# A graph layer on one core: spare rows gathered for two sets at once, 105 sets in place of 107, and another way to split x

## The chip, the core and the metric

The kernel runs on one core of a Trainium2 chip. The metric is the device time of one execution in microseconds (us): before the change the median of three runs is 1756.15 us (1748.27 to 1756.86). A profiled execution of the same kernel took 1757.87 us, and its span, from the first to the last instruction, is 1756.1 us.

The engines have short names in the profile. PE is the matrix engine (PEld its weight loads), DVE the vector engine, ACT the scalar engine, POOL the GpSimd engine. SP issues most DMA transfers, ACT and POOL issue some. An engine carries out its instructions strictly in the program's order, so an instruction that waits holds up everything behind it on its engine.

## The reference

```python
Xs = X[src]                                            # 400000 edges, 12500 nodes, 128 features
m_data = Xs @ W_data.T + b_data
m_ctrl = Xs @ W_control.T + b_control
msg = jnp.where((edge_types == 0)[:, None], m_data, m_ctrl)
agg = jax.ops.segment_sum(msg, dst, num_segments=X.shape[0])
out = relu(agg + (X @ W_self.T + b_self))
result = layernorm(X + out)
```

The edges are sorted by `dst`. Since the weights are the same for all edges of a type, the kernel sums the raw rows `X[src]` by destination and type first, and multiplies the sums by the weights afterwards.

## The kernel before, in words

**x in three parts.** Each f32 number of x is kept as three bf16 parts whose sum is the number, in SBUF as `x3` (128 partitions, 98 blocks, 3 parts, 128 features) and in DRAM as `rows3`. `split_x` makes the parts piece by piece, 14 blocks to a piece: ACT copies x to the first part (L262), DVE subtracts it from x (L263), ACT copies the rest to the second part (L264), DVE subtracts again into the third (L265). Seven full or nearly full pieces and one of 84 rows are made in the prologue. `store_rows` writes them to `rows3` (L269).

**Two ways to fetch rows.** The 3125 chunks of 128 edges fall into 25 groups of 125. Some chunks are *gathered*: an indirect DMA that POOL issues brings one `rows3` row per edge into a `msg` tile (`fetch`, L754). The others come in *sets* of 20 chunks (2560 edges) that PE serves: the edges are sorted into cells of 32 by the block of x in which their source lies, a 0/1 matrix `pick` is made, and PE multiplies it with `x3` (`pick`, L820) to get the rows; ACT brings them from PSUM to SBUF (`emsg`, L834). How many sets a group has is decided by `sets(g)`: five where g is a multiple of 4, else four, which makes 107 sets and 985 gathered chunks.

**Sums by destination.** For both kinds a 0/1 matrix (`psel`, `esel`, made by `select` on DVE, L504) says which destination and type a row belongs to, and PE multiplies (L704); counts go the same way (L842, L790). DVE adds a window of sums to the group's accumulator `acc` (L743). Finished tiles of 125 destinations are multiplied by the weights, normalized and written (`finish_batch`).

**A set in steps.** `give_slots` plans one set, ahead of its use: `block_matrix` (`O`, which block each edge's source is in), `fours` and `same_lane`, `before` (PE sums of who comes first, L584), `ranks` (each edge's place in its cell), `rank_matrix` (`rm`, `rv`), `over`, then `put` (L647), `spread` (the cells go through DRAM, `there`, and come back to all partitions as `pick`), `turn_codes` and `keep_codes`. `pick_matrix` turns the broadcast into the 0/1 matrix (L690). `picked` then works through the set in five turns: in each turn PE fetches four or five cells' rows (two in one PSUM tile, the rest in another), ACT evicts them, and PE counts and adds those of the turn before; `end` adds the last ones during the first turn of the next set.

**Spare rows.** A cell holds 32 edges. Edges over that, up to 64 a set, are *spare*: `over` finds them (up to seven a partition), `spare_slots` gives each a place: `over_before` (one PE matmul, L520), `over_matrix` (DVE, `om_all`, L526), `turn` (seven PE matmuls, L530), `keep` (three ACT copies, the last of which makes the row numbers `idx`, L541). `spare_rows` gathers these rows with one indirect DMA of 64 rows per set (L798) into the lower half of the tile `last`; its upper half takes the rows of two cells that are fetched by PE (L836). The last sum of the set reads `last`. The spare slots of set w are made while set w + 1 is planned, and the gather is issued in the second turn of set w.

**What sets the order.** The order of work on each engine is mostly written out: `merged` interleaves lists of units by numbers between 0 and 1. POOL's gathers are paced: `due` gives each a time in sets, and `paced` ties it to a matmul (a gate). 14 gathers run ahead (`AHEAD`), 18 `msg` tiles exist (`HOLD`). `issue_after` puts instructions behind a given one in their engine's order. The PSUM tile `side` exists once and is taken in turn by many steps.

**The prologue.** Before the first set can run, the tables are made, group 0 is loaded and prepared (`prep_e`), x is split, and sets 0 and 1 are planned. PE's first L820 starts at 68.00 us, POOL's first gather at 68.07 us.

Of the kernel before, what the change touches and what calls it, by code (L numbers as in the profile page):

```python
# [10 lines left out]
I32 = mybir.dt.int32  # L11
AF = mybir.ActivationFunctionType
# [138 lines left out]
def short_path(ctx, tc, const, ident, eps, wT, brow, bad, x, src, dst, etype, ws, bs, out):  # L151
# [24 lines left out]
    def sets(g):  # L176

        return NE if g % 4 == 0 else NE - 1
# [66 lines left out]
    def split_x(pool):  # L245
# [13 lines left out]
        def split(b, m, rows):  # L259
            t = tiles.pop(b)  # L260
            h, mm, lo = (x3[:rows, b:b + m, j, :] for j in range(3))
            nc.scalar.copy(h, t)  # L262
            nc.vector.tensor_sub(t, t, h)  # L263
            nc.scalar.copy(mm, t)  # L264
            parted.append(nc.vector.tensor_sub(lo, t, mm))  # L265
# [10 lines left out]
        for k, p in enumerate(pieces):  # L276
            def unit(k=k, p=p):
                split(*p)
# [25 lines left out]
    cell_col = keep.tile([P, NCELL], BF, name="cell_col")  # L304
    nc.vector.tensor_copy(cell_col.rearrange("p (a q) -> p a q", q=NQ), iota([4, NQ], [[1, 4], [4, NQ]], 0, 0, "i0"))
    for a, b in ((0, -1.0), (1, -1.0), (2, 96.0), (3, 97.0)):
        nc.vector.memset(cell_col[:, a * NQ + NQ - 1:a * NQ + NQ], b)
# [27 lines left out]
    om_all = keep.tile([P, TOP + 1, OVF], BF, name="om_all")  # L335
    nc.vector.memset(om_all, 0.0)
# [7 lines left out]
    for a in range(4):  # L344
        nc.vector.tensor_scalar(ltri[:, a, :], free[:, a, :], own_f[:, a:a + 1], None, op0=OP.is_gt)
# [10 lines left out]

    halves = tmp.tile([1, 2, NG * NE], I32, name="halves")
    nc.vector.memset(x3[:, NBLK - 1], 0.0)
    first = first_i["e"].rearrange("o g w -> o (g w)")
    nc.vector.tensor_single_scalar(halves[:, 0, :], first, 7, op=OP.logical_shift_right)  # L360
    nc.vector.tensor_single_scalar(halves[:, 1, :], first, 127, op=OP.bitwise_and)
# [12 lines left out]
    def places_and_weights():  # L374
        near = raw["near"] = keep.tile([rows_p, NG], FP, name="near")
        from_i = tmp.tile([rows_p, 1], I32, name="from_i")
        from_f = tmp.tile([rows_p, 1], FP, name="from_f")
        nc.gpsimd.iota(from_i, pattern=[[0, 1]], base=-PAD, channel_multiplier=DPC)
        nc.vector.tensor_copy(from_f, from_i)
        for k in range(1, NE):  # L380
            ge = raw[f"ge{k}"] = tmp.tile([rows_p, 1], FP, name=f"ge{k}")
            nc.vector.tensor_scalar(
                ge, from_f, float(DPC * PB * k - PAD), float(-DPC * PB), op0=OP.is_ge, op1=OP.mult
            )
        for k in range(1, NE):
            nc.vector.tensor_add(from_f, from_f, raw.pop(f"ge{k}"))
# [5 lines left out]
        least = tmp.tile([1, NG, NWIN], FP, name="least")  # L392
        for i, (_, _, c, _) in enumerate(windows(0)):
            nc.vector.memset(least[:, :, i:i + 1], float(max(0, c * DPC - PAD)))
# [80 lines left out]
    def prep_e(g):  # L475
# [17 lines left out]
        for v, val in enumerate((parts[:, 1, :], code)):  # L493
            nc.scalar.copy(vals2[:, :, v, :], val.rearrange("p (n o) -> p n o", o=1).to_broadcast([P, n, 2]))
        codes["e", g] = (blk, twice("blk2", parts[:, 0, :]), vals2, pk)

# [15 lines left out]
    def spare_slots(w, at):  # L512

# [3 lines left out]
        s = slots[w]  # L517

        def over_before():
            nc.tensor.matmul(  # L520
                at["ahead"][:, 500:501], ltri[:, 0, :], over_n[:, w:w + 1], start=True, stop=True, skip_group_check=True
            )

        def over_matrix():
            s["om"] = om_all.rearrange("p k o -> p (k o)")
            nc.vector.tensor_scalar(om_all[:, :TOP], slot_col, at["ahead"][:, 500:501], None, op0=OP.is_equal)  # L526

        def turn():
            for k in range(TOP):
# [719 lines left out]
```

## Time and profile before

| What | us |
|---|---|
| median of three runs | 1756.15 |
| profiled execution, its time | 1757.87 |
| its span | 1756.1 |
| ACT busy, of the span | 1229.2 (70%) |
| POOL, L754, 985 gathers of 128 rows, busy | 1190.9 |
| PE, L820, 10486 picks, busy | 568.0 |
| ACT, L834, 1070 evictions, busy | 951.9 |

How to read the rows that the prediction shows. A group of instructions is `line engine op out<-in shapes xcount | busy us, mean ns | idle before, and what ended it`. A timeline row is `start us, us, engine line op names xcount [idle before <-releaser]`; several like instructions in a row are merged, so that the time from one row's start to the next is what the engine spent on them. A row of the waits is `who waited <- for whom: us in total, times, longest us`. A row of a source line gives the count, then shortest, median and longest duration in ns, and the starts of the first and the last one. A row of the windows gives a stretch, its length and each engine's busy time in it, with the number of instructions that started there. Matmul ends are modelled and overlap; their starts are what counts.

### The profile page before, as it was taken

The page shows a single profiled execution, that of the slowest core. Times are in us where ns is not written, and L with a number is a line of the kernel's source. Part 1 is how long each engine was busy: PE and PEld are TensorE (multiplying, and loading weights), DVE is VectorE, ACT ScalarE, POOL GpSimd, SP SyncE. Part 2 cuts the span into 40 slices and gives each one's busy share as a digit, 9 for nine tenths or more (in the row PEclk, how much of TensorE's full clock was granted, in tenths as well). Part 3 has the DMA queues.
Part 4 walks back from the last instruction along what each step waited for, and adds up shares of the span by engine and source line. Part 5 has one row for each costly group of instructions (what it writes and reads, how often), then busy time and mean ns, then how long its engine had stood idle before and what let it go on. Part 6 is the DMA issues. An engine that isn't in the chain of part 4 may idle for free.

```text
span 1756.1 us, 72083 instructions
## 1 busy us (share of the span) xinstructions
PE 1615.3 (92%) x29945; PEld 1311.7 (75%) x29945; DVE 1595.2 (91%) x3996; ACT 1229.2 (70%) x2249; POOL 1316.6 (75%) x1109
## 2 busy tenths in 40 slices
PE   0599999999999999999999999999999989999997
PEld 0377777777778777777877877777777777878786
DVE  8899999998999998999988999999999989999993
ACT  4577777767677667767766777776777766767675
POOL 0288877787777787877887877887877877777871
PEclk9999999999999999999999999999999999999999
DMA  8655454446454545444535454544454535544441
GB/s 237 209 165 160 128 158 136 147 125 199 115 164 134 159 125 179 143 152 127 166 119 164 150 164 133 164 122 147 160 159 135 158 108 162 167 139 141 151 139 41
DMA packets 190562, 261.28 MB, mean 149 GB/s; under 512 B 86437, under 2 KB 155983, under 8 KB 187152
## 3 DMA queue, kind: packets, MB, share of 16 engines
q1 hardware_dynamic: 126894, 148.02, 25.9%
q0 software_dynamic: 50704, 102.16, 20.8%
q10 hardware_dynamic: 12626, 6.40, 1.2%
q8 instruction: 236, 3.87, 0.9%
q14 instruction: 102, 0.84, 0.1%
HBM read 238.47 MB, written 18.00 MB: 146 GB/s over the span
## 4 chain that ended last, share of the span: by engine, by line
PE 48%; DVE 32%; issue 6%; DMA 6%; ACT 5%; DVEq 1%; POOL 1%; SPq 0%; POOLq 0%; ACTq 0%
PE sums L704 22%; PE got L820 15%; DVE esel L504 3%; PE side L950 3%; DVE pick L690 3%; PE sums L842 3%; DMA last<-rows,idx 3%; DVE rv L635 2%; ACT emsg L834 2%; DVE prod L598 2%; DVE prod L576 2%; PE side L584 2%; DVE acc L743 2%; PE side L647 2%; DVE ahead L594 2%
## 5 line engine op out<-in xcount | busy, mean ns | idle before, releaser
L754 POOL DMA_INDIRECT msg<-rows,pidx x985 | 1190.9, 1209 | 307.5 <-issue 118.9
L834 ACT CAST emsg<-got 128x768 bf16<-128x768 f32 (+1 forms) x1070 | 951.9, 930 | 303.9 <-PE got L820 289.8
L704 PE MATMUL sums<-esel,emsg 128*128 128x176 bf16 x7704 | 683.4, 240 | 0.0
L704 PEld LDWEIGHTS <-emsg 128*128 128x128 bf16 x7704 | 566.9, 98 | 68.7 <-issue 28.5
L820 PE MATMUL got<-x,pick 128*32 128x384 bf16 x10486 | 568.0, 330 | 21.9 <-DVE pick L690 14.7
L820 PEld LDWEIGHTS <-pick 128*32 128x32 bf16 x10486 | 239.2, 96 | 139.2 <-issue 20.6
L504 DVE TENSOR_TENSOR esel<-code_col,code 128x1760 bf16<-128x1760 bf16 x321 | 292.7, 912 | 13.6 <-PE sums L704 11.6
L798 POOL DMA_INDIRECT last<-rows,idx x107 | 122.0, 1141 | 106.0 <-DVE pick L690 63.7
L704 PE MATMUL sums<-psel,msg 128*128 128x48 bf16 x2955 | 184.2, 184 | 17.2 <-DVE acc L743 15.2
L842 PE MATMUL sums<-esel,one_col 128*32 128x176 bf16 x2675 | 193.7, 240 | 4.4 <-DVE acc L743 4.4
L704 PEld LDWEIGHTS <-msg 128*128 128x128 bf16 x2955 | 149.9, 97 | 36.2 <-issue 31.4
L842 PEld LDWEIGHTS <-one_col 128*32 128x32 bf16 x2675 | 111.9, 97 | 60.7 <-issue 4.1
L790 PE MATMUL sums<-psel,one_col 128*128 128x48 bf16 x985 | 150.2, 183 | 0.0
L743 DVE TENSOR_TENSOR acc<-acc,sums 128x352 f32 (+2 forms) x232 | 99.4, 430 | 40.4 <-PE sums L704 36.8
L504 DVE TENSOR_TENSOR O<-cell_col,blk 128x2000 bf16<-128x2000 bf16 x107 | 128.2, 1198 | 2.1 <-issue 2.1
L598 DVE TENSOR_TENSOR prod<-O,ahead 128x2000 bf16<-128x2000 bf16 x107 | 127.6, 1193 | 0.1
L690 DVE TENSOR_SCALAR pick<-pick,lane_f 128x3200 bf16<-128x3200 bf16 x107 | 113.2, 1058 | 0.0
L647 PE MATMUL side<-rv,O 128*128 128x64 bf16 x2140 | 83.3, 195 | 31.6 <-DVE rv L635 30.6
L647 PEld LDWEIGHTS <-O 128*128 128x128 bf16 x2140 | 78.7, 100 | 33.3 <-DVE rv L635 29.3
L594 DVE TENSOR_REDUCE ahead<-side 128x100 bf16<-128x500 f32 x107 | 72.2, 675 | 28.0 <-PE side L520 27.3
L790 PEld LDWEIGHTS <-one_col 128*128 128x128 bf16 x985 | 94.3, 96 | 0.0
L635 DVE TENSOR_TENSOR rv<-rm,vals 128x1280 bf16<-128x1280 bf16 x107 | 87.8, 821 | 0.3
(170 smaller groups left out, 1869.2 us busy)
## 6 DMA issues: line engine op xcount, KB each, us to landing
pick<-there SPq DMA_DIRECT2D x107, 800.0 KB
acc<-acc_start SPq DMA_DIRECT2D x23, 1280.0 KB
msg<-rows,pidx POOLq DMA_INDIRECT x985
rows<-x SPq DMA_DIRECT2D x6, 1344.0 KB
xs<-in_x_dram SPq DMA_DIRECT2D x99, 62.5 KB
out_dram<-h SPq DMA_DIRECT2D x99, 62.5 KB
xt<-in_x_dram ACTq DMA_DIRECT2D x6, 896.0 KB
there<-cell SPq DMA_DIRECT2D x107, 6.2 KB
```

What stands on the lines that cost most here:

```text
L504: nc.vector.tensor_tensor(sel.rearrange("p n (w t) -> p n w t", t=2), col[:rows].rearrange("p (o w t) -> p o w t", o=1, t=2).to_broadcast( ...
L598: nc.vector.tensor_tensor(prod, s["O"], ahead.rearrange("p (o j) -> p o j", o=1).to_broadcast([P, EC, NCELL]), op=OP.mult)
L635: placed[:] = [nc.vector.tensor_tensor(rv.rearrange("p c v (r t) -> p c v r t", t=2), rm.rearrange("p c (o r t) -> p c o r t", o=1, t=2).t ...
L647: nc.tensor.matmul(s["rk"][:m, :2 * CAP], s["held"][:, c * NCELL:c * NCELL + m], s["rv"][:, c].rearrange("p v r -> p (v r)"), start=(c == ...
L690: nc.vector.tensor_scalar(t, t, lane_f, None, op0=OP.is_equal)
L704: last = nc.tensor.matmul(out, msg[:, j * D:(j + 1) * D], sel, start=(start and j == 0), stop=stop, skip_group_check=True)
L743: added.append(nc.vector.tensor_add(win, win, ps[:, :4 * wide].rearrange("p (a w) -> p a w", w=wide)[:, :, :width]))
L754: return nc.gpsimd.indirect_dma_start(out=msg, out_offset=None, in_=rows3[:, :], in_offset=bass.IndirectOffsetOnAxis(ap=codes["p", g][0][: ...
L790: nc.tensor.matmul(cnt, one_col, sel, start=False, stop=(c == n - 1), skip_group_check=True)
L820: last = nc.tensor.matmul(ps[CAP * a:CAP * (a + 1), :], slots[w]["pick"][:, a * NQ + q, :], x3[:, 4 * q + a - a0].rearrange("p j d -> p (j ...
L834: nc.scalar.copy(msg[:, :n], ps[:, :n, :3 * D])
L842: nc.tensor.matmul(cells_of(s["ps"], EW, 1)[CAP * (q % 4):CAP * (q % 4 + 1), :], one_col[:, :CAP], s["sel"][q], start=(q < 4), stop=(q + 4 ...
```

## The change

Five things change together.

1. `sets(g)` gives five sets where g is a multiple of 6, four elsewhere: 105 sets and 1025 gathered chunks.
2. The spare rows of two neighbouring sets, an even and the following odd one, come with one indirect DMA of 128 rows into `both`. The even set's spare slots are made as before; the odd set's are made from its own `rk` tile (`own_before`, `own_turn`). Of the even set, ACT copies its 64 rows from `both` to `last` at the end of the set's last turn; for the odd set `both` itself serves as `last`. The odd set has the halves of the tile, and the cells at its ends (`cell_cols`), the other way round. `both` and `last` have one buffer each.
3. x's parts are taken from its bytes: the upper two bytes of a f32 number are the first part, a bf16 number as they stand. ACT copies them, and copies the two lower bytes as numbers times 2^-15 and 2^-23; DVE masks sign and exponent out of the first part (`power`) and multiplies both other parts by it.
4. In the prologue, tables and the starting points of the gathered windows are made on DVE before the work that needs group 0's first loads; group 0's `prep_e` comes ahead of the split on ACT; the preparations of later groups stand behind `placed`.
5. The first set's two transfers `there` and `pick` are issued on POOL's queue.

```diff
-        return NE if g % 4 == 0 else NE - 1
+        return NE if g % 6 == 0 else NE - 1
...
-            h, mm, lo = (x3[:rows, b:b + m, j, :] for j in range(3))
-            nc.scalar.copy(h, t)
-            nc.vector.tensor_sub(t, t, h)
-            nc.scalar.copy(mm, t)
-            parted.append(nc.vector.tensor_sub(lo, t, mm))
+            part = x3[:rows, b:b + m]
+            byte = t.bitcast(U8).rearrange("p k (d b) -> p k d b", b=4)
+            nc.scalar.copy(part[:, :, 0, :], t.bitcast(BF).rearrange("p k (d b) -> p k d b", b=2)[:, :, :, 1])
+            for j in range(2):
+                nc.scalar.activation(part[:, :, 2 - j, :], byte[:, :, :, j], AF.Copy, scale=2.0 ** (8 * j - 23))
+            power = pool.tile([P, step, D], BF, name="power", bufs=2)[:rows, :m, :]
+            nc.vector.tensor_single_scalar(
+                power.bitcast(I16), part[:, :, 0, :].bitcast(I16), -128, op=OP.bitwise_and
+            )
+            parted.append(nc.vector.tensor_tensor(
+                part[:, :, 1:, :], part[:, :, 1:, :],
+                power.rearrange("p k (j d) -> p k j d", j=1).to_broadcast([rows, m, 2, D]), op=OP.mult,
+            ))
...
-    def spare_slots(w, at):
+    def spare_slots(w, at, col=504):
...
-        s = slots[w]
-
-        def over_before():
+        s, k = slots[w], w % 2
+        half = slice(k * OVF, k * OVF + OVF)
+        om = om_all[k]
+
+        def over_before(to="ahead", c=500):
+            s["before"] = at[to][:, c:c + 1]
...
-            spares = s["spares"] = spare_slots(w - 1, s)
+            spares = s["spares"] = spare_slots(w - 1 if w % 2 else -1, s)
...
+            queue = nc.sync if w else nc.gpsimd
+            queue.dma_start(out=there[:, :], in_=cell[:NCELL, :CAP])
...
+        def own_before():
+            s["own"] = spare_slots(w, s, 509)
+            s["own"][0]("rk", 508)
+            s["own"][1]()
+
+        def own_turn():
+            s["own"][2]()
+            s["own"][3]()
+
         s["tiled"] = {4: [put, spread], 5: [turn_codes, keep_codes]}
+        if w % 2:
+            s["tiled"][5] = [lambda: (turn_codes(), own_before()), keep_codes]
+            s["own_turn"] = own_turn
...
     def spare_rows(w):
-        msg = slots[w]["last"] = two.tile([P, 3 * D], BF, name="last")
+        n = P if w + 1 < pairs else OVF
+        both = two.tile([P, 3 * D], BF, name="both", bufs=1)
+        slots[w + 1 if n == P else w]["last"] = both
+        if n == P:
+            slots[w]["both"] = both
         return nc.gpsimd.indirect_dma_start(
-            out=msg[:OVF, :], out_offset=None, in_=rows3[:, :],
-            in_offset=bass.IndirectOffsetOnAxis(ap=slots[w]["idx"], axis=0),
+            out=both[:n, :], out_offset=None, in_=rows3[:, :],
+            in_offset=bass.IndirectOffsetOnAxis(ap=slots[w]["idx"][:n], axis=0),
         )
...
-            if t == 1 and w > 0:
+            if t == 1 and w > 0 and w % 2 == 0:
                 spare.append(lambda: spare_rows(w))
             if t == 3:
                 assert not spare
+                if "both" in slots[w]:
+                    slots[w]["last"] = two.tile([P, 3 * D], BF, name="last", bufs=1)
...
+            if t == 0 and w + 1 < pairs and "own_turn" in slots[w + 1] and w > 0:
+                slots[w + 1]["own_turn"]()
+            if t == turns - 1 and "both" in slots[w]:
+                nc.scalar.copy(slots[w]["last"][:OVF, :], slots[w]["both"][:OVF, :])
...
+    with tc.issue_after(tables.ins):
+        ready = prep_e(0)
     split_units.pop(0)()
-    prep_e(0)
```

More of the change, by code (lines that the diff above doesn't have):

```diff
@@ L344, in short_path @@
     for a in range(4):
[L345 removed]
+        tables = nc.vector.tensor_scalar(ltri[:, a, :], free[:, a, :], own_f[:, a:a + 1], None, op0=OP.is_gt)
     one_col = keep.tile([P, P], BF, name="one_col")
@@ new lines, in keep @@
+            nc.scalar.copy(
+                code, at["rk"][half, col + 2:col + 3].rearrange("p (n o) -> p n o", o=1).to_broadcast(list(code.shape))
+            )
+            part = two.tile([P, 2], FP, name="part")
+            nc.scalar.copy(part[half], at["rk"][half, col:col + 2])
+            if k == 0:
+                s["idx"] = two.tile([P, 1], I32, name="idx")
+            idx = slots[w - k]["idx"][half]
+            nc.scalar.activation(idx, part[half, 0:1], AF.Identity, bias=part[half, 1:2], scale=128.0)
@@ L1064, in ending, with later @@
         pass
+    def later(g):
+        with tc.issue_after(placed[0].ins):
+            prep_e(g)
     for w in range(pairs):
```

106 lines of the change are left out of this document (56 added, 50 removed).

## The prediction

> **What bounds the kernel now.** I read the page for the totals, then a window of the steady stage, then POOL's own timeline, then the waits.
>
> ```profile
> span 1756.1 us, 72083 instructions
> ...
> PE 1615.3 (92%) x29945; PEld 1311.7 (75%) x29945; DVE 1595.2 (91%) x3996; ACT 1229.2 (70%) x2249; POOL 1316.6 (75%) x1109
> ...
> L754 POOL DMA_INDIRECT msg<-rows,pidx x985 | 1190.9, 1209 | 307.5 <-issue 118.9 <-PE got L820 80.5 <-PE sums L704 51.9
> ```
> ```profile
> core 0: us, PE busy (x) PEld busy (x) DVE busy (x) ACT busy (x) POOL busy (x), PEclk, DMA share, GB/s
> 800.00:1000.00 200.00, 190.94 (x3583) 155.77 (x3576) 184.38 (x466) 142.73 (x267) 160.68 (x130) 1.00 0.48 144
> ```
> ```profile
> 889.76 1.04 POOL L754 DMA_INDIRECT msg<-rows,pidx  x1 [0.30 <-PE got L820]
> 891.10 3.51 POOL L754 DMA_INDIRECT msg<-rows,pidx  x1 [0.30 <-PE sums L704]
> 894.92 3.01 POOL L798 DMA_INDIRECT last<-rows,idx  x1 [0.30 <-ACT emsg L834]
> 898.24 0.95 POOL L754 DMA_INDIRECT msg<-rows,pidx  x1 [0.30 <-issue]
> ...
> 900.09 0.40 PE L704 MATMUL sums<-esel,last 128*128 128x176 bf16 x3 [3.04 <-DMA last<-rows,idx]
> ...
> 895.02 1.84 ACT L834 CAST emsg<-got 128x768 bf16<-128x768 f32 x2
> ...
> 900.69 0.20 ACT L677 CAST code<-side 128x50 bf16<-128x50 f32 x1 [3.83 <-PE side L530]
> ```
> ```profile
> PE sums L704 <- DMA last<-rows,idx: 15.2, 11, 4.5
> ```
>
> By its busy share POOL looks free (75%). It isn't. In the timeline every gather starts 0.30 us after the one before has ended, whichever releaser is named. In the 200 us window POOL has 130 gathers: 130 x 0.30 = 39 us of pauses and 160.7 us of work make 199.7 of 200 us. So POOL runs back to back, with PE at 95% and DVE at 92% beside it: three engines that are nearly equally full. What ties PE to POOL is the spare gather (`last`): when POOL lags, it lands late and PE stands still, as at 900.09 for 3.04 us; there were 11 such waits, 15.2 us in all. A change must lighten all three to gain its full worth.
>
> **The change, part by part.**
>
> *Sets and chunks.* Sets go from 107 to 105 (groups of five sets: 7 of 25 before, 5 of 25 after), chunks that POOL gathers from 985 to 1025. Gathers of spare rows go from 107 with 64 rows to 52 with 128 rows and one with 64.
>
> ```profile
> L754 POOL DMA_INDIRECT msg<-rows,pidx x985: 942/1043/4798, 73.2 to 1720.5; - x197
> ```
> ```profile
> L798 POOL DMA_INDIRECT last<-rows,idx x107: 911/1059/3007, 68.1 to 1729.9; - x107
> ```
> ```profile
> L798 POOL DMA_INDIRECT last<-rows,idx x107 | 122.0, 1141 | 106.0 <-DVE pick L690 63.7 <-issue 17.7 <-ACT idx L541 11.5
> ```
>
> POOL: 985 + 107 = 1092 slots become 1025 + 53 = 1078. If all take the mean of a 128-row gather, 1.209 us, busy time goes from 1190.9 + 107 x 1.14 (122.0 us) = 1312.9 to 1303.3, -9.6 us, and 14 pauses of 0.30 fall away, -4.2: together -14 us. If a wide spare gather is no dearer than a narrow one (the medians, 1059 ns for 64 rows and 1043 for 128, say so), 14 average slots of 1.50 go: -21 us.
>
> The spread of `msg` (0.94 to 4.8 us for the same 128 rows) is no cost of the gather alone. The Trainium skill ("SBUF — State Buffer", section "SBUF: two separate sides") says that VectorE's two-port instructions and GpSimd exclude each other from a shared port, so that descriptors which GpSimd writes must wait. By that rule only the shortest time is the gather's own, 14 x (0.94 + 0.30) = 17.4 us are saved by count, and the rest of POOL's time belongs to VectorE's work by set, 2 sets of it: (1312.9 - 1092 x 0.94) / 107 x 2 = 5.4 us, -22.7 us in all by this estimate. The 3.51 us gather above agrees with waiting of some kind, but names no port.
>
> PE: one set's matmuls are read from starts in the timeline.
>
> ```profile
> 808.06 1.00 PE L820 MATMUL got<-x,pick 128*32 128x384 bf16 x20
> 808.88 0.32 PE L842 MATMUL sums<-esel,one_col 128*32 128x176 bf16 x5
> 809.13 0.41 PE L584 MATMUL side<-prod,ltri 128*128 128x125 bf16 x4
> ...
> 809.41 1.30 PE L704 MATMUL sums<-esel,emsg 128*128 128x176 bf16 x15
> 810.54 0.24 PE L704 MATMUL sums<-psel,msg 128*128 128x48 bf16 x3
> ...
> 810.83 1.00 PE L820 MATMUL got<-x,pick 128*32 128x384 bf16 x20
> ```
>
> 20 picks take 0.82 us to the next start, so 98 take 4.0; 5 counts 0.25, so 25 take 1.25; 15 sums 1.13, so 75 take 5.65; the ranks 0.28. That is 11.2 us a set, without a few small groups. Two gathered chunks take 810.83 - 810.54 = 0.29, so 0.145 each. Two sets fewer and 40 chunks more: -22.4 + 5.8 = -17 us.
>
> DVE: the selections and masks that exist once a set:
>
> ```profile
> L504 DVE TENSOR_TENSOR esel<-code_col,code 128x1760 bf16<-128x1760 bf16 x321 | 292.7, 912 | 13.6 <-PE sums L704 11.6
> ...
> L504 DVE TENSOR_TENSOR O<-cell_col,blk 128x2000 bf16<-128x2000 bf16 x107 | 128.2, 1198 | 2.1 <-issue 2.1
> L598 DVE TENSOR_TENSOR prod<-O,ahead 128x2000 bf16<-128x2000 bf16 x107 | 127.6, 1193 | 0.1
> L690 DVE TENSOR_SCALAR pick<-pick,lane_f 128x3200 bf16<-128x3200 bf16 x107 | 113.2, 1058 | 0.0
> ```
>
> These four alone are 661.7 / 107 = 6.2 us, and many smaller ones come on top, so two sets are worth more than 12 us; the window's 184.4 us are 14.5 a set (sets follow each 15.7 us: L798's first and last start, 106 steps apart), so two are at most 29 us. All three engines fall by 12 to 29 us; I take **-19 us** for the steady stage.
>
> ```profile
> L836 ACT CAST last<-got 64x384 bf16<-64x384 f32 x107 | 50.7, 474 | 2.6
> ```
>
> *One gather for two sets.* The odd set's row numbers are now made at the end of the set two earlier (`own_before`) and in the next set's first turn (`own_turn`): the same seven matmuls, the same mask on DVE (its place is now behind the esel and O above, some 2.2 us, and PE's turn queues behind it), the same three ACT copies, later than before. POOL's gather waits for them; behind it queue the `msg` gathers. While POOL lags, its wait is covered by that lag; if it has none, it isn't the bound at that place. Cost 0; without that cover up to 52 waits of 0.2 us, 10 us. The new ACT copy `last<-both` (64x384) is nearest to L836's 474 ns: 52 x 0.47 = 24.6 us on an engine that is 30% idle, hidden unless it waits (a rival below). `both` and `last` in one buffer each: the next gather is gated one turn after its last reader, so nothing.
>
> *The prologue.* Its rows:
>
> ```profile
> L263 DVE TENSOR_TENSOR xt<-xt,x 128x1792 f32<-128x1792 f32 x6 | 12.1, 2014 | 0.0
> ...
> L262 ACT CAST x<-xt 128x1792 bf16<-128x1792 f32 x6 | 10.0, 1681 | 0.0
> ```
> ```profile
> 9.04 0.22 DVE L360 TENSOR_SCALAR halves<-first_e 1x125 int32<-1x125 int32 x1 [6.03 <-DMA edst<-in_dst_dram]
> ...
> 13.48 0.87 DVE L345 TENSOR_SCALAR ltri<-i,own_f 128x128 bf16<-128x128 int32 x4
> ...
> 48.47 1.89 DVE L263 TENSOR_TENSOR xt<-xt,x 128x1664 f32<-128x1664 f32 x1 [2.66 <-ACT x L262]
> ...
> 52.89 2.02 DVE L265 TENSOR_TENSOR x<-xt,x 128x1792 bf16<-128x1792 f32 x1 [2.53 <-ACT x L264]
> ...
> 65.03 0.33 SPq L269 DMA_DIRECT2D rows<-x  x1
> ...
> 66.91 1.03 DVE L690 TENSOR_SCALAR pick<-pick,lane_f 128x3200 bf16<-128x3200 bf16 x1
> ...
> 71.26 1.95 DVE L504 TENSOR_TENSOR esel<-code_col,code 128x1760 bf16<-128x1760 bf16 x2
> ...
> 73.22 0.98 POOL L754 DMA_INDIRECT msg<-rows,pidx  x1 [2.19 <-ACT pcol L450]
> ```
>
> DVE is the path up to the first mask at 66.91. A piece of x costs it 2 x 2.01 = 4.03 us now. After, it costs a product of 3584 bf16 elements and a bit mask of 1792 16-bit ones. The product is like L598, 2000 in 1.193: 3584 x 0.596 = 2.1 us; at L263's rate it would be 4.0. The mask, a single-source 16-bit instruction like L690 (3200 in 1.058): 0.6 us; at L263's rate 2.0. I take the fast ends, 2.7 us, as both rows share type and layout; the bounds are 2.7 and 6.0. Seven pieces and a rest: -9.4 us (slow: +14). The Trainium skill ("VectorE: DVE Perf Modes", section "The perf-mode tier table") gives 693 ns for a 2048-element bf16 single-source instruction and half that speed for two sources; it speaks of bf16 for the first, no row here shows int16, and by it the sum is the fast one.
>
> ACT goes from two copies a piece to three, 3 x 1.68 = 5.0 us (a byte source has no row; I bound it by 1.68 and twice that). From about 14 us that is 36 us and some small copies and a wait for `bits`: it ends near 57, just under DVE. At twice the price for the two byte copies it would end near 80 and hold everything, some 20 us later than taken.
>
> The tables (up to 13.48 + 0.87) move into the 6.03 us in which DVE waited for its first loads: -3 us. The waits of 2.66 and 2.53 on ACT go since DVE no longer feeds ACT's second copy: -5. Set 2's `O` now stands ahead of the mask: +1.2. Set 0's two transfers through POOL's queue leave SP's; POOL does nothing then. Altogether the mask comes some 12 us earlier, at about 55 (the sum of these terms is 16; I leave 4 for ACT's waits). The last store of `rows`, held on SP behind set 1's `there` until 65.03, follows the last product at about 60. The first esel (71.26) and POOL's stream (73.22) are behind the last products, `psf` and the ids, which now come after the mask: about 8 us earlier. I take **-8**, with 0 and -13 as bounds at fast rates.
>
> **Sum:** 1756.1 - 19 - 8 = 1729 us of span. The profiled execution's time was 1757.87, 1.8 us over its span; the runs' median, 1756.15, is 1.7 below that time, so 1729 stands for the median too.
>
> **Rivals.**
> - *PE freed from POOL.* POOL loses at the upper end and starts earlier, so `last` lands in time: the 15.2 us of waits go as well, of which I count 14: 1715. For it: odd sets' rows now come one set early. Against: even sets need theirs sooner, at the ACT copy.
> - *The split runs at the slow rates.* DVE pays 6.0 a piece, +14 - 3 - 5 + 1 = +7 instead of -8, partly behind the loads: 1729 + 13 = 1742. For: neither form is in the trace.
> - *Slower: ACT waits for the spare rows.* Place: `last<-both` in the last turn of each even set, in ACT's order ahead of the next set's `emsg`. At 895.02 ACT would have ended its last eviction at 896.86 and sat until the rows landed near 900, where it now waits 3.83 us for PE anyway. Price: such a wait in each of 52 even sets at the mean of those seen, 15.2 / 11 = 1.4 us, is +73: 1802. It decides from 0.7 us a pair (36 us, which brings it above 1764). Against: only 11 waits in 107 sets, and most gathers land earlier.
> - *The steady stage doesn't follow.* Fewer slots and sets, but the rest (acc, masks) keeps PE at its pace and the prologue's gain is eaten by the same three engines later: -5 of 27 remains, 1751. Against: PE, DVE and POOL all lose work in that stage.
>
> **Chances.** Forecast 0.55, PE freed 0.14, slow rates 0.12, ACT waits 0.10, not followed 0.09. About 0.5% (8.8 us: under 1747.4 or over 1764.9) can be told from no change. Faster: 0.55 + 0.14 + 0.09 of slow rates + 0.01 = 0.79. Same: 0.03 of slow rates, 0.02 of ACT waits, 0.08 = 0.13. Slower: 0.08. The forecast's own range is 1718 to 1742; with PE freed and the unfollowed case it becomes 1708 to 1757, which leaves out the ACT case and the far ends.
>
> **What would show it.** Gathers still 0.30 us apart and about 1078 of them; wide gathers near 1.0 to 1.2 us; the first mask near 55 and POOL's first `msg` near 65; `power` at 0.6 and the product at 2.1 us; ACT's byte copies at 1.68. Wrong it would be made by a product at 4 us, by ACT rows that wait on DMA `both`, by PE waiting on `om_all`, or by pauses on POOL that wait for `idx`.

## The result, and the profile after

The changed kernel takes 1869.81 us (median of six runs, 1862.71 to 1876.52), the kernel before 1754.22 beside it: a ratio of 1.066, 95% interval 1.062 to 1.070. The forecast was 1729, so it missed by 141 us and in sign. The profiled execution took 1876.52 us.

The experiments ran on several chips. On one (the first four runs) the kernel before takes 1754.6 us; on two others (all later runs) it takes 2075 to 2101, and PE has long waits there for which the profile names no cause. Ratios are always to the kernel before on the same chip, and microseconds are compared within one group only. Single disturbed executions (2979 us of the kernel before, 2125 and 6877 us of the kernel with the copy behind turn 3) are not counted.

The page of the changed kernel: span, busy time by engine, then groups (busy and mean ns, idle time ahead of them and what ended it).

```profile
span 1874.8 us, 71581 instructions
...
PE 1646.9 (88%) x29637; PEld 1320.6 (70%) x29637; DVE 1577.4 (84%) x3948; ACT 1243.3 (66%) x2275; POOL 1271.4 (68%) x1097
...
L789 POOL DMA_INDIRECT msg<-rows,pidx x1025 | 1206.7, 1177 | 461.9 <-PE sums L739 158.9
...
L862 PE MATMUL got<-x,pick 128*32 128x384 bf16 x10290 | 587.0, 334 | 105.9 <-ACT emsg L876 89.3
...
L929 ACT COPY last<-both 64x384 bf16<-64x384 bf16 x52 | 26.6, 512 | 146.2 <-DMA both<-rows,idx 146.2
```

PE has 308 matmuls fewer than before (29945) and is busy 31.6 us longer. POOL, which ran back to back before, now waits for PE. One group stands out: the new ACT copy works for 26.6 us, and ACT stands still ahead of it for 146.2. The steady window and the waits (us in total, times, longest) say the same.

```profile
800.00:1000.00 200.00, 181.90 (x3287) 146.56 (x3287) 170.39 (x431) 132.78 (x245) 145.48 (x121) 0.97 0.44 136
```
```profile
POOL msg L789 <- PE sums L739: 158.9, 236, 4.9
ACT last L929 <- DMA both<-rows,idx: 146.2, 51, 10.2
...
DVE esel L521 <- PE sums L739: 100.9, 50, 9.2
...
PE got L862 <- ACT emsg L876: 89.3, 76, 8.7
```

All four engines do less in the 200 us than before (PE 190.94, DVE 184.38, ACT 142.73, POOL 160.68), so none of them is the bound; a wait is. 51 of the 52 copies waited, 2.87 us each on the mean. PE's wait of picks for evictions (`emsg`) is 89.3 us now; before it was 5.8:

```profile
L820 PE MATMUL got<-x,pick 128*32 128x384 bf16 x10486 | 568.0, 330 | 21.9 <-DVE pick L690 14.7 <-ACT emsg L834 5.8 <-ACT vals L494 0.2
```

One pair shows how it goes (timeline: start, duration, instruction, idle time before it).

```profile
518.33 0.29 ACT L564 ACTIVATE idx<-part 64x1 int32<-64x1 f32 x1
518.64 1.82 ACT L876 CAST emsg<-got 128x768 bf16<-128x768 f32 x2
...
519.34 0.95 POOL L837 DMA_INDIRECT both<-rows,idx  x1 [0.30 <-issue]
...
520.65 1.00 PE L862 MATMUL got<-x,pick 128*32 128x384 bf16 x20
...
523.57 0.51 ACT L929 COPY last<-both 64x384 bf16<-64x384 bf16 x1 [3.11 <-DMA both<-rows,idx]
...
523.99 1.80 ACT L876 CAST emsg<-got 128x768 bf16<-128x768 f32 x2
...
524.83 0.51 PE L862 MATMUL got<-x,pick 128*32 128x384 bf16 x8 [1.24 <-ACT emsg L876]
...
525.90 1.51 ACT L876 CAST emsg<-got 128x768 bf16<-128x768 f32 x2
527.43 0.47 ACT L878 CAST last<-got 64x384 bf16<-64x384 f32 x1
```

The row numbers are ready at 518.62, the gather is issued at 519.34, and its rows are used at 523.57, 3.28 us after POOL has done with it. ACT meanwhile has two evictions to do, ends them at 520.46 and then stands at the copy, though PE's next twenty picks have been done since 521.65. PE fills its free buffers, and its next picks wait from 523.59 to 524.83. In the code the copy is the last thing of turn 4. In ACT's built order it stands elsewhere. Only turn 3 has the eviction `last<-got`, at 527.43 here, so the two evictions at 525.90 are turn 3's and those at 523.99 turn 2's: this copy stands behind turn 1's evictions, three turns early. Counted over the trace, 27 of the 52 copies stand there, 11 between turn 2's two evictions, 13 behind both, and only the first set's stands behind all ten evictions of its set; it is the one that did not wait.

The prologue, on DVE, ACT and POOL:

```profile
15.82 3.28 ACT L267 ACTIVATE x<-xt 128x1792 bf16<-128x1792 uint8 x2
16.35 0.62 DVE L269 TENSOR_SCALAR power<-x 128x1792 int16<-128x1792 int16 x1
20.15 2.02 DVE L272 TENSOR_TENSOR x<-x,power 128x3584 bf16<-128x3584 bf16 x1
...
31.04 0.35 DVE L434 CAST part<-brow 1x384 bf16<-1x384 f32 x1 [7.75 <-DMA edst<-in_dst_dram]
...
61.03 1.05 DVE L725 TENSOR_SCALAR pick<-pick,lane_f 128x3200 bf16<-128x3200 bf16 x1
...
65.35 0.28 DVE L272 TENSOR_TENSOR x<-x,power 84x256 bf16<-84x256 bf16 x1
...
74.98 1.04 POOL L837 DMA_INDIRECT both<-rows,idx  x1 [23.95 <-DMA ptyp<-in_edge_type_dram]
```

Each new instruction costs what was forecast, and the first mask comes at 61.03 (66.91 before). But the last part of x is done at 65.63 (60.37 before), and POOL's first gather starts at 74.98 (68.07 before).

### The profile page after: what moved, and what is told of

It is laid out like the page before. It is cut to its first block, busy times and chain, and to the rows that moved or that the text cites. A ratio compares the mean times of both kernels' runs of the same rounds, so it can differ in the third digit from the quotient of the medians.

```text
span 1874.8 us, 71581 instructions
## 1 busy us (share of the span) xinstructions
PE 1646.9 (88%) x29637; PEld 1320.6 (70%) x29637; DVE 1577.4 (84%) x3948; ACT 1243.3 (66%) x2275; POOL 1271.4 (68%) x1097
## 4 chain that ended last, share of the span: by engine, by line
PE 37%; DVE 23%; issue 13%; DMA 10%; ACT 7%; POOL 6%; DVEq 1%; SPq 0%; POOLq 0%; ACTq 0%
PE sums L739 16%; PE got L862 11%; DMA both<-rows,idx 9%; POOL msg L789 6%; ACT emsg L876 5%; PE side L998 3%; DVE esel L521 3%; PE sums L884 2%; DVE pick L725 2%; DVE prod L620 2%; DVE rv L657 2%; PE side L669 1%; DVE prod L598 1%; DVE ahead L616 1%; DVE prod L625 1%
## 5 line engine op out<-in xcount | busy, mean ns | idle before, releaser
L789 POOL DMA_INDIRECT msg<-rows,pidx x1025 | 1206.7, 1177 | 461.9 <-PE sums L739 158.9
L876 ACT CAST emsg<-got 128x768 bf16<-128x768 f32 (+1 forms) x1050 | 934.5, 928 | 325.4 <-PE got L862 316.1
L739 PE MATMUL sums<-esel,emsg 128*128 128x176 bf16 x7560 | 691.9, 244 | 0.7 <-ACT emsg L876 0.7
L862 PE MATMUL got<-x,pick 128*32 128x384 bf16 x10290 | 587.0, 334 | 105.9 <-ACT emsg L876 89.3
L862 PEld LDWEIGHTS <-pick 128*32 128x32 bf16 x10290 | 241.6, 96 | 228.2 <-issue 116.9
L521 DVE TENSOR_TENSOR esel<-code_col,code 128x1760 bf16<-128x1760 bf16 (+2 forms) x315 | 288.0, 914 | 103.6 <-PE sums L739 100.9
L739 PEld LDWEIGHTS <-msg 128*128 128x128 bf16 x3075 | 158.4, 98 | 30.3 <-issue 28.6
L929 ACT COPY last<-both 64x384 bf16<-64x384 bf16 x52 | 26.6, 512 | 146.2 <-DMA both<-rows,idx 146.2
L669 PE MATMUL side<-rv,O 128*128 128x64 bf16 (+1 forms) x2100 | 83.1, 196 | 30.9 <-DVE rv L657 30.7
L837 POOL DMA_INDIRECT both<-rows,idx x53 | 59.6, 1125 | 71.2 <-ACT idx L564 35.9
L669 PEld LDWEIGHTS <-O 128*128 128x128 bf16 (+1 forms) x2100 | 78.8, 101 | 32.9 <-DVE rv L657 30.6
```

Of the source, the lines that this page charges most:

```text
L521: nc.vector.tensor_tensor(sel.rearrange("p n (w t) -> p n w t", t=2), col[:rows].rearrange("p (o w t) -> p o w t", o=1, t=2).to_broadcast( ...
L669: nc.tensor.matmul(s["rk"][:m, :2 * CAP], s["held"][:, c * NCELL:c * NCELL + m], s["rv"][:, c].rearrange("p v r -> p (v r)"), start=(c == ...
L739: last = nc.tensor.matmul(out, msg[:, j * D:(j + 1) * D], sel, start=(start and j == 0), stop=stop, skip_group_check=True)
L789: return nc.gpsimd.indirect_dma_start(out=msg, out_offset=None, in_=rows3[:, :], in_offset=bass.IndirectOffsetOnAxis(ap=codes["p", g][0][: ...
L862: last = nc.tensor.matmul(ps[CAP * a:CAP * (a + 1), :], slots[w]["pick"][:, a * NQ + q, :], x3[:, 4 * q + a - a0].rearrange("p j d -> p (j ...
L876: nc.scalar.copy(msg[:, :n], ps[:, :n, :3 * D])
```

## Experiments on the chip where the kernel before takes 1754.6 us

**The copy moved.** It is issued behind the last eviction of turn 4, where the prediction had put it. The texts on record for this run and the next call the old place "behind turn 2's evictions", which holds for 13 of the 52 copies, and the rows the odd set's; the copy brings the even set's.

```diff
-            nc.scalar.copy(msg[:, :n], ps[:, :n, :3 * D])
+            s["out"] = nc.scalar.copy(msg[:, :n], ps[:, :n, :3 * D])
...
-                nc.scalar.copy(slots[w]["last"][:OVF, :], slots[w]["both"][:OVF, :])
+                with tc.issue_after(s["out"].ins):
+                    nc.scalar.copy(slots[w]["last"][:OVF, :], slots[w]["both"][:OVF, :])
```

> The changed kernel with one thing moved: ScalarE's copy of the odd set's spare rows is issued behind the last eviction of turn 4 of the even set, where the prediction had put it, and not right behind turn 2's evictions. Theory P (place): the copy stood in front of turn 3's evictions and waited for its gather 51 times of 52 (146.2 us); moved two turns on it finds its rows landed, ScalarE's wait there falls under 10 us, TensorE's wait for evictions (89.3 us) falls under 15, and the time is 1720 to 1750. Rival C (chain): the rows of the odd set come too late in any place, since the row numbers, the gather and its landing hold the lane of GpSimd's queue: the wait of the copy shrinks but GpSimd's pauses stay, 1790 to 1850. Rival K (clock): the lower granted clock of TensorE (0.973 against 0.995) is a cost of the new split or of the even sets and not of the stalls: 1760 to 1790 with the clock still near 0.97.

Measured: 1757.5 us (ratio 1.0019, interval 1.0007 to 1.0030). Of its page and its waits:

```profile
span 1755.4 us, 71589 instructions
...
PE 1607.3 (92%) x29637; PEld 1290.4 (74%) x29637; DVE 1573.1 (90%) x3948; ACT 1242.4 (71%) x2275; POOL 1309.3 (75%) x1097
...
L789 POOL DMA_INDIRECT msg<-rows,pidx x1025 | 1245.6, 1215 | 324.1 <-issue 128.3
```
```profile
POOL msg L789 <- issue: 128.3, 421, 0.3
...
POOL msg L789 <- PE got L862: 71.3, 228, 0.8
POOL msg L789 <- PE sums L739: 69.0, 194, 4.1
...
ACT last L930 <- DMA both<-rows,idx: 14.3, 8, 5.6
...
PE got L862 <- ACT emsg L876: 9.7, 26, 1.0
```

One instruction moved by two to three turns takes 112 us off. ACT's wait at the copy falls from 146.2 to 14.3 us (8 copies still wait, a little more than theory P's 10 us), PE's for evictions from 89.3 to 9.7. The same 29637 matmuls keep PE busy 39.6 us less, and TensorE's mean granted clock is 0.996 against 0.973: the lower clock came with the stalls, so rival K falls. POOL is back at pauses of 0.30 to 0.36 us on the mean (128.3 / 421, 71.3 / 228, 69.0 / 194), so rival C falls too. But theory P's range, 1720 to 1750, is missed: the mended kernel is no faster than the one before.

**The copy without its wait.** It reads x's own parts; the even sets' spare rows are left out.

```diff
-                nc.scalar.copy(slots[w]["last"][:OVF, :], slots[w]["both"][:OVF, :])
+                nc.scalar.copy(slots[w]["last"][:OVF, :], x3[:OVF, 0].rearrange("p j d -> p (j d)"))
```

> The changed kernel with the copy where it stands, behind turn 2's evictions, but reading rows that have long been in SBUF (x's own parts) in place of the merged gather's: it waits for no transfer, and the odd sets' spare rows are left out. Theory P: what costs is the wait inside the copy and not the copy: ScalarE waits under 5 us there, time within 10 us of the run with the copy moved (1715 to 1750). If the copy's own 0.51 us in front of an eviction is a cost too, it is 10 to 25 us above the moved one. Rivals C and K as in the run with the copy moved: 1790 to 1850, or 1760 to 1790 with a clock near 0.97.

The built order moved with the edit: in the trace 40 of the 52 copies now stand behind the first turn of the odd set before, earlier still than in the changed kernel.

Measured: 1751.28 us (0.9983, 0.9971 to 0.9995), within 10 us of the run with the copy moved and 1.3 above the range; ACT waits 3.2 us in all at the copy. So 52 copies ahead of other evictions cost nothing that shows when they do not wait. With the run before, which takes most of the wait away and 112 us with it, the loss lies in the wait inside the copy. The changed kernel's very place without the wait was not run.

**The sets alone**, in the kernel before: `g % 4` becomes `g % 6` in `sets`.

> The kernel before with the sets alone changed: five and six experts by turns of six, so 105 sets and 1025 chunks; each set keeps its own gather of spare rows and the old split. By the prediction's terms a steady saving of 18 to 19 us less the share that the merged gather had in it (52 gathers of GpSimd, about 52 times 1.5 us, stay): GpSimd has 1025 + 105 gathers in place of 1078, so if GpSimd bounds the sets, little is won, 1740 to 1758; if TensorE does (fewer matmuls, 11.2 us a set), 1725 to 1740. Over 1780 would say that the sets themselves cost the time lost.

Measured: 1788.8 us (1.0196, 1.0172 to 1.0220), above every range but the last clause: two sets fewer, with their 40 chunks more, make the kernel *slower* by 34 us. Its waits, then two of its groups:

```profile
PE sums L704 <- DMA last<-rows,idx: 53.0, 22, 6.7
```
```profile
L754 POOL DMA_INDIRECT msg<-rows,pidx x1025 | 1223.3, 1193 | 316.3 <-issue 119.5 <-PE got L820 73.3 <-PE sums L704 57.6
L798 POOL DMA_INDIRECT last<-rows,idx x105 | 121.4, 1156 | 101.4 <-DMA bias<-b_parts 64.4 <-issue 18.9 <-ACT idx L541 6.5
```

POOL has 38 gathers more. Busy time on gathers is 1344.7 us against 1312.9 before, +32, and 38 pauses of 0.30 are +11. PE's wait for the spare rows, which tells how far POOL lags, goes from 15.2 to 53.0 us, and that is about the loss on this chip.

**The split alone**, in the kernel before: the six lines of `split_x` from the change and nothing else of it.

> The kernel before with the split of x alone changed: ScalarE copies the bytes, VectorE masks and multiplies. Prediction: 8 us in the prologue, 1743 to 1750. From the trace of the changed kernel, whose first mask came 6 us earlier and not 12 and whose first messages came 3 us later: 1750 to 1762. Rival K (the split slows what follows, by clock or otherwise): over 1770.

Measured: 1752.95 us (0.9991, 0.9976 to 1.0006): nothing that can be told from zero, as the changed kernel's trace had suggested; not the forecast 8 us, and no loss either.

## Experiments where the kernel before takes 2075 to 2101 us

**107 sets, merged gather, copy late** (`g % 6` back to `g % 4` in the run with the copy moved).

> The run with the copy moved, with the sets of before put back (107 sets, 985 chunks): so the merged gather and the new split without the change of sets. GpSimd then has 985 + 54 gathers, 53 fewer than before, and 39 fewer than with 105 sets; TensorE has its 107 sets again. Theory G (GpSimd's gathers set the sets' pace, 1.5 us for each with its pause): up to 39 x 1.5 = 58 us under the run with the copy moved, of which TensorE's and VectorE's own work, 92% and 90% busy there, leave some 15 to 30: 1715 to 1742. Rival T (fewer sets are a gain in any case, as the prediction took it; what is missing is lost by the merged gather's chain): 1760 to 1780, slower than the 105 sets.

Measured: 2049.9 us beside 2100.88 (0.9751, 0.9718 to 0.9784). The sign is theory G's, but on this chip POOL is busy only 60% of the span, so the run can't speak for G. Three repeats, all on chips of this kind:

> The 107 sets with the merged gather, the new split and the late copy, once more: on the chip of its first run every kernel was some 20% longer (before 2100.88 us), with TensorE waiting on its own instructions, so that the gathers could not be the bound there. Theory G (GpSimd's gathers at 1.5 us each set the pace; 53 fewer than before): where before takes about 1754, this takes 1715 to 1740 (ratio 0.978 to 0.992). Rival T (fewer sets are a gain in any case): 1760 to 1780.

> 107 sets, merged gather with the late copy, new split. Theory G (GpSimd's gathers at 1.5 us each set the pace where before takes 1754): 53 gathers fewer than before, 1712 to 1735, below the 105 sets by 20 us or more. Rival T (fewer sets are a gain in any case): 1760 to 1780.

> 107 sets, merged gather with the late copy, new split. Where before takes about 1754: theory G (the gathers' count sets the pace) 1712 to 1735; rival T (fewer sets are a gain in any case) 1760 to 1780. Where before takes 2075 to 2100: again a ratio of 0.972 to 0.983.

Measured: 0.9772, 0.9773 and 0.9775 (intervals together 0.972 to 0.983); a fourth repeat stands below. Only the last of these texts has a range for a kernel before of 2075 to 2100 us, and that range holds. Rival T, by which 107 sets are slower than 105, does not show here: 105 sets take 0.991 below. How this kernel does where before takes 1754 stays untried.

**Bias casts late** (105 sets, copy late).

```diff
-    bparts()
+    with tc.issue_after(parted[5].ins):
+        bparts()
```

> The run with the copy moved (105 sets), and VectorE's casts of the bias parts issued behind the sixth part of x and not ahead of it. In the run before VectorE stood 8.06 us at 31.30 for the bias rows' load, the last part of x was done at 65.89, and GpSimd's first gather began at 75.20 (before: 60.37 and 68.07). Theory B: the wait goes, the last part is done near 58, the first gather begins near 67, and the time falls by the same 6 to 8 us: 1748 to 1753. Rival D: the transfers set the prologue's end (the row stores at 340 to 370 GB/s from 56 on), the first gather stays at 72 to 75 and the time within 3 us of 1757.

Measured: 2081.18 us (0.9915, 0.9885 to 0.9944). Of its timeline:

```profile
45.07 2.02 DVE L272 TENSOR_TENSOR x<-x,power 128x3584 bf16<-128x3584 bf16 x1 [2.56 <-ACT x L267]
...
63.41 0.27 DVE L272 TENSOR_TENSOR x<-x,power 84x256 bf16<-84x256 bf16 x1
...
75.70 1.21 POOL L837 DMA_INDIRECT both<-rows,idx  x1 [24.36 <-DMA bias<-b_parts]
```

DVE's 8 us wait for the bias row is gone, and DVE waits for ACT's byte copies instead; the last part gains 2 us and the first gather none, which is rival D's side (75.70, just over its 72 to 75). The DMA traffic fits it: the core moves 319 to 365 GB/s from 56 to 72 us here and 342 to 372 in the run with the copy moved, and only 126 and 110 from 72 to 76, when the first gather starts. No run shows apart what the stores and what ACT's copies hold up. Both edits together, on the same chip as the run with 107 sets, gave 2051.63 us (0.9757, 0.9729 to 0.9786) beside that run's 2049.90: the late casts are worth nothing.

> Both of the two runs beside it: merged gather with the late copy, new split with late bias casts, and the 107 sets of before. If theories G and B hold the two add up: 1708 to 1736, under the kernel before by 1 to 2.5%. If G's rival holds, 1752 to 1775; if only B fails, within 4 us of the run with 107 sets.

The repeat of the late casts gave 0.9907 (0.9869 to 0.9945):

> 105 sets, copy behind turn 4, the bias casts behind the sixth part of x. On another chip VectorE's 8.06 us wait was gone, but the last part of x ended at 63.68 (65.89 with the early casts), held by ScalarE's three byte copies of each part, and the first gather stayed at 75.70. So the prologue's bound has moved from VectorE to ScalarE and the stores: 1752 to 1760, within 4 us of the run with the copy moved (1757.5). If the earlier mask alone counted: 1745 to 1750.

**The merged gather with the split of before**: 107 sets, copy late, and the split of before put back. The text calls it the merged gather alone; parts 4 and 5 of the change, the prologue's order and its queue, are still in it.

> The merged gather alone, with its copy late: the sets of before (107) and the split of before. Theory G: the gather pairs carry the whole gain, so within 5 us of the run beside it, 1715 to 1742. If the new split is worth its predicted 8 us after all, this is 6 to 10 us slower than the run beside it; if the new split costs (first gather at 75 in place of 68), 4 to 8 us faster.

Measured: 0.9741 (0.9683 to 0.9799); again: 0.9782 (0.9742 to 0.9822). Beside the five values with the new split (0.9751 to 0.9775) the split is worth nothing here either, and the gain comes with the merged gather. Parts 4 and 5 do not start the work sooner (first picks at 68.3 and 68.5 us, first `msg` at 74.6 and 74.1, against 68.2 and 73.4 with the sets alone on such a chip), but no run has the merged gather without them.

> 107 sets, merged gather with the late copy, the split of before: the merged gather alone. Theory G: within 6 us of the run beside it; 3 to 8 us under it if the new split, whose last part of x comes 5 us later and whose first gather 7 us later, costs there what it delays.

**The copy behind turn 3** (105 sets; `issue_after` names the eighth eviction in place of the last).

> The changed kernel with the copy behind turn 3's evictions: one turn later than in the changed kernel, one earlier than in the run with the copy moved. Theory P (a wait of 2.87 us each behind turn 2, none two turns on; the rows land about 3.3 us after the gather starts, a turn takes some 3 us): ScalarE waits for few pairs, under 0.6 us each on the mean (30 us in all), and the time is within 15 us of the run with the copy moved, 1750 to 1772. If the loss were that the copy stands ahead of any eviction, and not its wait, 1800 or more.

> 105 sets, the copy behind turn 3's evictions. Theory P (the wait in the copy is the cost): ScalarE's wait there under 30 us in all, time 1750 to 1775. If standing ahead of an eviction were the cost in itself: 1800 or more.

Measured: 0.9905 (0.9877 to 0.9934) and 0.9921 (0.9895 to 0.9947), with no wait for the rows above 0.1 us in the trace of the first. On these chips turn 3 is late enough (in the pair above the rows were used 4.2 us after the gather's start, 3.3 after its end), and evictions may well stand behind the copy. The times on record are for a kernel before of 1754 us and stay untried.

**The changed kernel itself**, on such a chip:

> The changed kernel as it is, beside the run with 107 sets. Where before takes about 1754: 1.062 to 1.070 again. Where before takes 2075 to 2100 and TensorE is the slow one, each turn is longer (about 17%), so the row has more time to land behind turn 2's evictions, but a late eviction stands directly on TensorE's path: 1.02 to 1.05 by theory P; 1.06 or more if the wait does not shrink with the longer turns.

Measured: 1.0013 (0.9982 to 1.0045), below the range of theory P. Its waits, first of PE's weight loads (116.9 us in the changed kernel on the first chip), then of ACT's copy:

```profile
PEld L862 <- issue: 210.1, 396, 3.1
...
ACT last L929 <- DMA both<-rows,idx: 64.7, 37, 3.6
```

The copy waits 37 times instead of 51, for 64.7 us. Moving it is worth 1% here (0.9905 and 0.9921 behind turn 3), against 6% on the first chip: each wait is 64.7 / 37 = 1.7 us instead of 2.87. That longer turns cover part of the transfer and PE's other waits part of the stall is likely, but not shown.

**Sets alone and 107 sets**, side by side:

> 107 sets, merged gather with the late copy, new split. Where before takes about 1754: theory G (40 gathers fewer than with 105 sets) 1712 to 1735; rival T (fewer sets are a gain in any case) 1760 to 1780. Where before takes 2075 to 2100: a ratio of 0.972 to 0.983, as three times before.

> The kernel before with 105 sets alone. Where before takes about 1754: 1.017 to 1.022 again. Where before takes 2075 to 2100 and GpSimd is idle 40% of the time: if GpSimd's 38 gathers more are all that the sets cost, they are hidden there and TensorE's saving of 1% shows, 0.985 to 1.000; if the 40 chunks cost as much on TensorE's own path, 1.01 to 1.02 there too, as the mended kernel's 0.991 (105 sets) against 0.977 (107) says.

Measured: 0.9772 (0.9724 to 0.9821) and 1.0138 (1.0099 to 1.0177). So the sets cost 1.4% here too, where POOL is busy 63% and its extra gathers should have been hidden. GpSimd's lag, shown as PE's wait for rows on the first chip, is not the whole cause. The value lies in the second range on record (the 40 chunks cost as much on TensorE's own path), but no row shows where PE would pay that.

## Why the prediction failed, step by step

*The ACT copy's place: the step that failed, 112 us.* The prediction priced this very wait as its slower rival (1802, chance 0.10) but put the copy "in the last turn of each even set, in ACT's order ahead of the next set's `emsg`", and took its time as "hidden unless it waits". All but the first stand two to three turns earlier, with turn 2's or turn 3's evictions right behind them, and 51 of 52 wait. Moved to the foreseen place: 1757.5; early without the wait: 1751; early with it: 1870. The rival's price was too small as well: 2.87 us a pair instead of 1.4. That price came from PE's waits for rows in the kernel before; here row numbers, gather and use follow each other within 5.3 us (518.33 to 523.57). Its own point of decision, 0.7 us a pair, was passed four times over.

*The steady stage, -19: nothing came.* PE was to fall by 17 us and fell by 8.0 (1615.3 to 1607.3 with the copy moved). The price of 0.145 us a chunk was read rightly: in the kernel before, these rows stand between the `psel` row at 810.54 and the picks at 810.83, so the 0.29 us hold two chunks, each of three matmuls and a count.

```profile
810.62 0.18 PE L790 MATMUL sums<-psel,one_col 128*128 128x48 bf16 x1
810.64 0.23 PE L704 MATMUL sums<-psel,msg 128*128 128x48 bf16 x3
810.72 0.18 PE L790 MATMUL sums<-psel,one_col 128*128 128x48 bf16 x1
```

What the sum left out is PE's share in the merged gather, put at 0. Count in the traces from each matmul's start to the next one's start, or to its own end where PE then stood. The picks and the sums of `emsg` fall by 23.0 us and the chunks rise by 2.0 (0.157 us each before, 0.152 after). But three other groups rise by 15.7: the counts of the sets from 129.6 to 137.4, the sums that read `last` or `both` from 24.6 to 29.1, the seven matmuls of the spare places from 20.3 to 23.7. With the sets alone (129.1, 25.6, 20.2) and with the split alone (129.0, 24.4, 20.2) they hardly change, so the rise comes with the merged gather.

POOL's term (-14 to -21) counted 14 gathers fewer, and there are 14 fewer. The spare ones with the copy moved:

```profile
L837 POOL DMA_INDIRECT both<-rows,idx x53 | 58.7, 1107 | 51.4 <-DMA ptyp<-in_edge_type_dram 23.9 <-ACT idx L564 12.5 <-issue 10.7
```

Busy time on gathers went from 1312.9 to 1245.6 + 58.7 = 1304.3, -8.6; 14 pauses are -4.2. Against that stand the later first `msg` (76.54 against 73.22, +3.3) and the idle time ahead of `msg` beyond 0.30 us each, which goes from 307.5 - 985 x 0.30 = 12.0 to 324.1 - 1025 x 0.30 = 16.6, +4.6. The sum is -5 (the span fell by 0.7). Sums of this size are not sure: the 1092 gathers of the kernel before took 1176.3 + 124.2 = 1300.5 us in the run with the split alone, 12 us less than in the kernel before.

DVE's term (-12 to -29) was right: with the sets alone it is -18.0 (1595.2 to 1577.2). But that kernel is slower, so DVE alone does not set the time.

The larger fault is one of method: two parts that pull against each other were booked as one count. The merge takes 54 gathers away, the sets add 40. By themselves the sets cost 2.0% on the first chip. That the merge and its cover won this back is worked out and not run: 1.0019 / 1.0196 = 0.983, with a split that is worth nothing.

The Trainium skill's rule ("SBUF — State Buffer", section "SBUF: two separate sides") would have had POOL's time above its shortest gather fall with DVE's work. At the prediction's 0.94 us each, 1304.3 - 1078 x 0.94 = 291 us were above it with the copy moved, 1312.9 - 1092 x 0.94 = 286 before, though DVE did 22 us less. But the run with the split alone has 1300.5 - 1092 x 0.94 = 274 with the gathers of before, so two traces differ by more than the 5.4 us at stake, and no run here decides it.

*The merged gather at cost 0:* apart from the copy and from PE's share above, near it. With the copy moved, POOL's gather waited for `idx` three times, 12.5 us in all (the group above), against a bound of 10 and against 11.5 us before.

*The prologue, -8: -1.6 measured with the split alone, within zero.* The prices were right: mask 0.62, product 2.02, byte copies 3.28 / 2 = 1.64. Of the 12 us by which the first mask was to come earlier 6 came. DVE stood 7.75 us for the bias row, whose casts now stand early in its order (the row names the load of `edst`; the instruction reads `brow`). That wait does not explain the rest: with it gone the first mask came at 60.02, against 61.29 with the copy moved. What failed is that POOL's stream would start "about 8 us earlier". The last part of x is done 5 us later than before, the store behind it is issued 2.7 us later (67.75 against 65.03), and POOL's first gather starts at 74.98 against 68.07. With DVE's wait taken away, DVE waited for ACT, which spends 1.68 + 3.28 = 5.0 us on a piece where it spent 2 x 1.68 = 3.4, and the gather did not move (75.70 against 75.20 with the copy moved).

*The signs that were listed:* "ACT rows that wait on DMA `both`" is the row that shows the cause; PE's waits on `om_all` are 4.8 us in the changed kernel, as good as nothing; POOL's pauses for `idx` are 35.9 us there and 12.5 with the copy moved.

What stays open: why two sets fewer with 40 chunks more cost 1.4% where POOL has time to spare, where the merged gather's 15.7 us on PE come from, and whether 107 sets with the merged gather, 2.2 to 2.6% faster than before in eight runs, are as much faster where before takes 1754 us.

## What to carry to other kernels

An edit that adds an instruction which consumes a transfer puts a wait into an engine's order: read from the built order, not from the code, what stands right behind it, and count the time from the transfer's issue to that place. Rows that land 3.28 us after their gather has ended, as in the pair above, do not fit behind two evictions of 0.9. When a change both removes and adds work of one kind, price the two apart, each with its own run; here a loss of 2% and a gain of about as much were booked as one small gain.

## What the runs showed of the hardware that had not been expected

- Stalls cost twice. Between the changed kernel and the one with the copy moved the span differs by 119.4 us: PE's idle time by 79.8, and its busy time for the same matmuls by 39.6, at a granted clock of 0.973 against 0.996 (1607.3 x 0.996 / 0.973 = 1645, against 1646.9 measured). The Trainium skill ("TensorE: Matmul & The Clock Gate", section "HAM oscillation — how this bites in real kernels") says that idle gaps over about 3.4 us bring PE back to half its clock. The direction agrees, but here shorter gaps went with it too: in the trace of the changed kernel the granted clock falls to half 23 times, 102 us in all (twice, 15 us, with the copy moved), and at 18 of the 23 PE had no gap above 3.4 us in the 7 us before, counted from the modelled ends of its matmuls. In the 3.4 us just ahead of each it had stood 1.7 us or more in all.
- The same kernel takes 20% longer on some chips (before: 2075 to 2101 us against 1754), and the granted clock accounts for little of it (0.962 to 0.979 against 0.992 to 0.997). With the sets alone, PE's weight loads of `pick` waited 17.2 us on the first chip and 217.5 on another for nothing that the profile names (`PEld L820 <- issue: 17.2, 76, 0.6` and `PEld L820 <- issue: 217.5, 404, 2.0`). On such a chip the loss from the copy's wait shrinks from 6% to 1%, so a verdict from one chip did not hold on the other.
- ACT copies bytes (uint8 to bf16, 1792 in 1.64 us) at the price of f32 (1.68), and DVE's 16-bit integer mask runs at 1792 in 0.62 us.
